# The start of a recursive matrix kernel: fewer warm-up products, whole-tile normalising, and another order of transposes, copies and sums

## The chip, the cores and the metric

The kernel runs on one core of a Trainium2 chip. Its metric is the device time of one execution in microseconds (us), the median of several runs. The core has five engines that run side by side, each through its own list of instructions in order: TensorE multiplies matrices (in the profile PE, with the loads of its stationary operand apart as PEld), VectorE (DVE) and ScalarE (ACT) compute element by element and can read TensorE's result banks in PSUM, GpSimd (POOL) computes on SBUF only, and SyncE (SP) issues the transfers between HBM and SBUF. An engine that waits for another holds everything behind it in its own list.

## The reference

The input x is 2 x 1024 tokens of 512 values, in float32. What is computed, cut to its core:

```python
xn = layernorm(x)                          # no weights, eps 1e-5
s = einsum('bsk,nk->bsn', xn, weight * block_mask)        # 512 x 512, blocks of 32 x 32
nx = xn * rsqrt(mean(xn**2) + 1e-5) * ln_w
h = silu(einsum('bsh,ih->bsi', nx, gate_w)) * einsum('bsh,ih->bsi', nx, up_w)   # 1792 rows each
ffn = einsum('bsi,hi->bsh', h, down_w)
out = x + s * silu(ffn)
```

## The kernel before, in words

The tokens are cut into four groups t of 512; each group is four tiles i of 128 tokens x 512 values. A tile is loaded with the tokens on the partitions, normalised there, and turned by TensorE in 128 x 128 pieces: `transpose(t, c, i)` turns chunk c (128 of the 512 values) of tile i into a quarter of the bank `pt[t, c]`. A full bank is copied to SBUF by ScalarE (`evacuate`, L163) and is then an operand, `raw[c, t]`, of 128 x 512. For a float32 product of 128 x 512 the trace shows two matmul records, 0.43 us apart.

Products are saved by two levels of a Strassen-Winograd scheme. The outer level makes seven block instances q out of a large product, each inner instance seven products m of 128 x 512 instead of eight. The operands 1, 2 and 3 are data as they are; the operands 5, 6, 7 and 4 are differences, made for the tokens by `inner_b` (for instances 1 and 2 of the first stage by VectorE straight out of the banks `pt[1, c]`) and for the weights by `inner_a` on GpSimd. Products are accumulated in the banks x, y and z of an instance; `seed`, `snap` and `total` (L350 to L373) copy or add what stands in them at given points, partly on ScalarE, partly on VectorE. A bank can only be written on when it has been read: so a copy or a sum decides when TensorE may go on.

There are eight groups g of weights: seven of gate and up weights, each 256 rows, and one of the masked weights. The instances 1 and 2 of all groups come first. They need only the tokens of t = 0 and 1, and so instance j = 0 (g 0, q 1) and j = 1 (g 0, q 2) start as soon as these are ready. Then come the instances 6, 5, 7, 3 and 4 of all groups, and at last the product with the down weights.

No scheduler decides the order. Every piece of work is entered by `at(pos, function, arguments)` with a position by hand; at the end the list is sorted by position and written out, so each engine's order is the order of the positions. A position is a slot of TensorE in the steady stream; instance j has the slots 7j and on, and `T(us)` turns an estimated time at the start into a position. `EARLY` holds positions of the first products (j, m) and of totals (j, "z") that differ from the rule; (j, 0) is the position of `seed`. The framework adds the waits that the data and the banks ask for, and between two engines that use one bank also where both only read: the one that comes later in the order waits.

The start, in the order of the code: SP loads tiles t = 0, weights of group 0, tiles t = 1, weights of group 1, and so on. TensorE is kept busy with products of an identity matrix that nobody reads (`warm`, L702). VectorE takes the statistics of each tile (L125, L126), works out a factor and an offset per token (`factors`: L139, a square root on ScalarE at L140, a reciprocal L136 and L137), and normalises tiles 2 and 3 in place (L146) while ScalarE does tiles 0 and 1 (L148), each in two halves of 256 columns. Then come transposes, copies and the first products for t = 0, and the same for t = 1. GpSimd multiplies the weights of group 0 by ln_w (L262) and forms their sums (L97, the helper `add`, which stands for sums on every engine). For group 1 ScalarE does this multiplication (`scale_a`, L264).

Of the kernel before, what the change touches and what calls it, by code (L numbers as in the profile page):

```python
# [15 lines left out]
W = 512  # L16
# [15 lines left out]
def tile_masked_linear_gated_ffn(  # L32
# [33 lines left out]
    EARLY = {}  # L66

    def at(pos, fn, *args):
        events.append((pos, len(events), fn, args))
# [23 lines left out]
    def bank(tag, name):  # L93
        return ps.tile([P, W], F32, tag=tag, name=name, bufs=PSB[tag])
# [4 lines left out]
    dve, pool, act = nc.vector, nc.gpsimd, nc.scalar  # L99
# [28 lines left out]
    def factors(t):  # L128


        scl = small.tile([P, TT], F32, tag="scl", name=f"scl_{t}")
        nb = small.tile([P, TT], F32, tag="nb", name=f"nb_{t}")
        stat[t] = (scl, nb)

        def last():
            nc.vector.reciprocal(scl, scl)  # L136
            nc.vector.scalar_tensor_tensor(nb, agg[:, t, :, 0], -1.0, scl, ALU.mult, ALU.mult)  # L137

        return [lambda: nc.vector.tensor_scalar(scl, agg[:, t, :, 1], 1.0 + EPS, EPS * EPS, ALU.mult, ALU.add),  # L139
                lambda: nc.scalar.activation(scl, scl, AF.Sqrt), last]  # L140
# [443 lines left out]
    def down_instance(o, q, where_, prior, dest, after):  # L584
# [78 lines left out]
        if last_set:  # L663
            at(where_(17) + 0.1, base_of_last)
            for part, pos in zip(parts, (where_(23), where_(24), where_(25))):
# [8 lines left out]
    where = {gq: j for j, gq in enumerate(order)}  # L674
    N = len(order)
    END = 7 * N
    T = lambda us: (us - 14.0) / 0.86
    EARLY.update({(0, 1): T(10.4), (0, 2): T(11.3), (1, 1): T(12.1), (1, 2): T(13.0), (0, 0): T(11.5), (1, 0): 4.3,
                  (0, "z"): 3.26, (1, "z"): 4.9})
    SILU = 26.2  # L680
    at(T(-10), constants)
    at(T(-10), load_x, 0)
    at(T(-10), lambda: nc.scalar.dma_start(lnw_sb, ln_w))

    at(T(-10), lambda: nc.gpsimd.tensor_copy(mem[:, F["a1"], 0:1], xt[0, 0][:, 0:1]))
    for K in range(2):
        at(T(-10), load_a, 0, K)
    at(T(-10), load_x, 1)
# [6 lines left out]
    def plan(pos, step, todo):  # L695
        for i, fn in enumerate(todo):
            at(pos + step * i, fn)


    def warm(n, b):  # L700
        for _ in range(n):
            nc.tensor.matmul(b[:, :P], ident, ident, start=True, stop=True, skip_group_check=True)  # L702

    at(T(1.4), lambda: warm(26, bank("V", "idle")))
    for t, p, step in ((0, T(7.1), 0), (1, T(12.5), 0), (2, 36.0, 1.2), (3, 36.1, 1.2)):
        plan(p, step, factors(t))
    for i in range(TT):
        half = act if i < 2 else dve
        at(T(3.7 + 0.82 * i), stats, 0, i)
        at(T(9.35 + 0.82 * i), stats, 1, i)  # L710
        for h, cols in enumerate((slice(0, W // 2), slice(W // 2, W))):
            at(T(7.95 + 0.9 * h + 0.4 * (i % 2)), normalise, 0, i, half, cols)
            at(T(13.45 + 0.9 * h + 0.4 * (i % 2)), normalise, 1, i, half, cols)
        for c in range(KC):
            at(T((8.9, 9.3, 9.8, 11.0)[c] + 0.05 * i), transpose, 0, c, (2, 3, 0, 1)[i], "XYYX"[c])
            at(T((14.35, 14.8, 15.25, 16.2)[c] + 0.05 * i), transpose, 1, c, (2, 3, 0, 1)[i], "XVVV"[c])
    at(T(6.0), scale_a, 0, 0, pool)
    at(T(6.1), scale_a, 0, 1, pool)
    for c in range(KC):
        at(T((9.75, 10.3, 10.85, 12.05)[c]), evacuate, 0, c, act)  # L720
        at((5.6, T(15.6), 6.0, 3.14)[c], evacuate, 1, c, act)
    for pos, q, m, eng in ((1.1, 1, 5, dve), (1.87, 1, 6, dve), (2.56, 1, 7, dve), (3.95, 2, 5, dve), (2.7, 1, 4, pool),
                           (4.6, 2, 6, dve), (7.2, 2, 7, dve), (5.0, 2, 4, pool)):
        at(pos, inner_b, q, m, eng)
    for q in (1, 2):
        for k in (0, 1):
            for n in (0, 1):
                at(8, outer_b, q, k, n, None)
    at(2.1, scale_a, 1, 0)
    at(5.2, scale_a, 1, 1)  # L730
    for i in range(TT):
        at(14.0 + 2.5 * i, stats, 2, i)
# [28 lines left out]
    for g in range(G + 1):  # L761
        p, rest = 7 * where[g, 1], 7 * where[g, BLOCKS[0]]
# [43 lines left out]
    def D(o):  # L806
        return lambda k: free[25 * o + k] if 25 * o + k < 25 * len(DOWN) else free[25 * o + k - 1] + 1
# [6 lines left out]
    for o, q in enumerate(DOWN):  # L814
# [24 lines left out]
        for k in range(4):  # L839
            pos = END + (-6, -4.8, 2, 4)[k] if o == 0 else D(o - 1)(10) + 2.5 * k  # L840
# [84 lines left out]
```

## Time and profile before

| | us |
|---|---|
| median of 3 runs (513.14 to 514.0) | 513.15 |
| profiled execution | 513.17 |
| span of its trace | 511.4 |
| TensorE busy in the span | 505.8 (99%) |
| VectorE | 380.4 (74%) |
| GpSimd | 340.9 (67%) |
| ScalarE | 182.6 (36%) |

The profile is of one execution. A row of the timeline gives the start and the length, both in us, the engine and the line of the code, the operation with its output and input, and in brackets how long the engine stood idle before it and who ended that. Several instructions of a kind that follow each other are put in one row (x4). A row of busy time by stretch gives the stretch, its length, and for PE, PEld, DVE, ACT and POOL the busy time and the number of instructions, then the clock that TensorE was granted, the busy share of the transfer engines, and GB/s.

### The profile page before, as it was taken

What the parts mean: (1) busy time and instruction counts of PE and PEld (TensorE: products, weight loads), DVE (VectorE), ACT (ScalarE), POOL (GpSimd) and SP (SyncE); (2) the same over time, 40 slices, a digit from 0 to 9 for tenths busy, and PEclk for the clock granted to TensorE, in tenths of its full rate; (3) what the DMA queues carried; (4) which work ended last, traced back from release to release, by engine and by line L of the source; (5) the groups of instructions that cost most, each with busy time, mean ns of one, the idle gap of its engine ahead of it and who ended that gap; (6) DMA issues with size and microseconds to landing.
All of it is one profiled execution on the core that took longest, in us unless ns stands there. A gap on an engine that the chain in (4) does not pass through costs nothing. (4 is left out here: it accounts for less than half of the span.)

```text
span 511.4 us, 4943 instructions
## 1 busy us (share of the span) xinstructions
PE 505.8 (99%) x1269; PEld 231.8 (45%) x1269; DVE 380.4 (74%) x590; ACT 182.6 (36%) x348; POOL 340.9 (67%) x283
## 2 busy tenths in 40 slices
PE   8999999999999999999999999999999999999997
PEld 8444444444444444444444444444444444444444
DVE  6878689876977969699696978968747645367736
ACT  4656754633536353353634433330100101001111
POOL 5522224994795968869597789976662754739960
PEclk9999999999999999999999999999999999999999
DMA  8436636369159386785948667499997698476472
GB/s 289 164 132 238 247 133 227 135 236 350 48 219 348 147 302 228 238 289 208 338 166 294 209 239 254 169 332 383 357 339 270 204 374 327 146 252 216 151 229 83
DMA packets 60460, 121.59 MB, mean 238 GB/s; under 512 B 5760, under 2 KB 13328, under 8 KB 58384
## 3 DMA queue, kind: packets, MB, share of 16 engines
q1 hardware_dynamic: 60288, 121.27, 66.8%
q8 instruction: 10, 0.16, 0.1%
q14 instruction: 18, 0.15, 0.1%
q10 hardware_dynamic: 144, 0.00, 0.0%
HBM read 75.11 MB, written 46.15 MB: 237 GB/s over the span
## 5 line engine op out<-in xcount | busy, mean ns | idle before, releaser
L97 POOL TENSOR_TENSOR mem<-mem 128x512 f32<-128x512 f32 (+4 forms) x245 | 305.2, 1267 | 135.4 <-ACT mem L264 36.5
L343 PE MATMUL x<-mem 128*128 128x512 f32 x448 | 213.6, 595 | 0.2 <-DVE mem L97 0.2
L343 PEld LDWEIGHTS x<-mem 128*128 128x128 f32 x448 | 83.7, 190 | 107.3 <-issue 86.9
L97 DVE TENSOR_TENSOR mem<-x,mem 128x512 f32<-128x512 f32 x137 | 92.5, 684 | 42.0 <-PE x L343 41.1
L343 PE MATMUL y<-mem 128*128 128x512 f32 x224 | 114.5, 593 | 0.3 <-DVE mem L97 0.3
L97 DVE TENSOR_TENSOR mem<-mem 128x512 f32<-128x512 f32 (+3 forms) x60 | 74.7, 1252 | 7.8 <-PE dx L591 4.3
L591 PE MATMUL dx<-mem 128*128 128x512 f32 x174 | 78.3, 592 | 0.0
L97 DVE TENSOR_TENSOR mem<-y,mem 128x512 f32<-128x512 f32 x96 | 65.6, 684 | 9.8 <-PE y L343 8.5
L343 PEld LDWEIGHTS y<-mem 128*128 128x128 f32 x224 | 42.2, 190 | 53.0 <-issue 47.8
L350 ACT COPY z<-x 128x512 f32<-128x512 f32 x54 | 30.9, 573 | 97.9 <-PE x L343 92.2
L343 PE MATMUL z<-mem 128*128 128x512 f32 x112 | 57.3, 593 | 0.0
L591 PEld LDWEIGHTS dx<-mem 128*128 128x128 f32 x174 | 33.1, 190 | 41.6 <-issue 40.4
L591 PE MATMUL dy<-mem 128*128 128x512 f32 x98 | 44.5, 592 | 0.0
L409 ACT ACTIVATE gate<-mem 128x512 f32<-128x512 f32 x56 | 33.1, 601 | 25.3 <-DVE mem L97 20.9
L414 DVE TENSOR_TENSOR mem<-gate,mem 128x512 f32<-128x512 f32 x56 | 38.0, 681 | 5.1 <-POOL mem L97 4.3
L564 POOL TENSOR_TENSOR mem<-mem 128x512 f32<-128x512 f32 x16 | 25.0, 1570 | 15.3 <-DMA mem<-s_dram 15.2
L343 PEld LDWEIGHTS z<-mem 128*128 128x128 f32 x112 | 21.0, 190 | 24.9 <-issue 23.9
L574 ACT ACTIVATE silu<-mem 128x512 f32<-128x512 f32 x15 | 9.0, 602 | 64.6 <-DVE mem L97 48.3
L97 DVE TENSOR_TENSOR mem<-z,mem 128x512 f32<-128x512 f32 x41 | 28.0, 682 | 3.5 <-PE z L343 3.5
L591 PEld LDWEIGHTS dy<-mem 128*128 128x128 f32 x98 | 18.6, 190 | 23.4 <-issue 23.4
L97 DVE TENSOR_TENSOR mem<-dx,mem 128x512 f32<-128x512 f32 x16 | 11.0, 690 | 20.1 <-PE dx L591 20.1
L591 PE MATMUL dz<-mem 128*128 128x512 f32 x56 | 25.2, 592 | 0.0
(73 smaller groups left out, 289.2 us busy)
## 6 DMA issues: line engine op xcount, KB each, us to landing
h_dram<-mem SPq DMA_DIRECT2D x98, 256.0 KB, 2.1
mem<-h_dram SPq DMA_DIRECT2D x28, 768.0 KB, 6.2
mem<-in_gu SPq DMA_DIRECT2D x42, 256.0 KB, 3.7
acc_dram<-mem SPq DMA_DIRECT2D x8, 1024.0 KB, 4.2
mem<-acc_dram SPq DMA_DIRECT2D x8, 1024.0 KB, 6.7
mem<-in_x SPq DMA_DIRECT2D x16, 256.0 KB, 5.2
s_dram<-mem SPq DMA_DIRECT2D x16, 256.0 KB, 4.8
mem<-s_dram SPq DMA_DIRECT2D x16, 256.0 KB, 6.3
```

What stands on the lines that cost most here:

```text
L97: eng.tensor_tensor(o, a, b, op)
L343: nc.tensor.matmul(st[key], weights(g, q, m), operand(q, m), start=first and not (key == "z" and seeded), stop=True, skip_group_check=True)
L350: nc.scalar.copy(st["z"], st["x"])
L409: nc.scalar.activation(gate[key], t(), AF.Silu)
L414: nc.vector.tensor_mul(a(), gate[key], b())
L564: at_later.append(lambda: nc.gpsimd.tensor_tensor(s_tile, s_tile, rms_bc[t], ALU.mult))
L574: nc.scalar.activation(b[0][:, part], y[:, part] if source is None else source(), AF.Silu)
L591: nc.tensor.matmul(st[key], w(), b(), start=first and key != "z", stop=True, skip_group_check=True)
```

## The change

Everything that changes is in the table of positions at the start; no function is changed.

- The identity products are 20 instead of 26.
- VectorE normalises tiles 2 and 3 of t = 0 and of t = 1 in one instruction each of 128 x 512, instead of two halves. ScalarE keeps its halves.
- For t = 0 the four chunks are transposed in a row; before, the first product stood between the third chunk and the fourth. Within chunks 0 and 1 the tiles are taken in the order 2, 0, 1, 3 (t = 0) or 0, 2, 1, 3 (t = 1) instead of 2, 3, 0, 1.
- For t = 1 the y product of instance 0 stands after chunk 1 instead of after chunk 2, and the x product m = 6 stands between chunk 2 and chunk 3.
- ScalarE: the copy of x of instance 0 (`seed`, L354) moves from between the third and the fourth copy of t = 0 to after the first copy of t = 1. The copy of chunk 3 of t = 1 moves behind the copy of x (L361), and is now later than the sum `inner_b(2, 6)` on the same bank; the first `scale_a` of group 1 moves behind the copy of y.
- VectorE: the z total of instance 0 moves ahead of the sum `inner_b(1, 7)`; the z total of instance 1 ahead of `inner_b(2, 6)`, right after the sum of x of instance 1 (`seed`, L356).
- The orders of GpSimd and of SP stay as they are.

```diff
-    T = lambda us: (us - 14.0) / 0.86
-    EARLY.update({(0, 1): T(10.4), (0, 2): T(11.3), (1, 1): T(12.1), (1, 2): T(13.0), (0, 0): T(11.5), (1, 0): 4.3,
-                  (0, "z"): 3.26, (1, "z"): 4.9})
+    T = lambda us: (us - 13.4) / 0.86
+    EARLY.update({(0, 1): T(10.2), (0, 2): T(11.1), (1, 1): T(12.0), (1, 2): T(12.9), (0, 0): 1.8, (1, 0): 4.3,
+                  (0, "z"): 2.5, (1, "z"): 4.6})
...
-    at(T(1.4), lambda: warm(26, bank("V", "idle")))
-    for t, p, step in ((0, T(7.1), 0), (1, T(12.5), 0), (2, 36.0, 1.2), (3, 36.1, 1.2)):
+    at(T(1.4), lambda: warm(20, bank("V", "idle")))
+    for t, p, step in ((0, T(7.1), 0), (1, T(12.2), 0), (2, 36.0, 1.2), (3, 36.1, 1.2)):
         plan(p, step, factors(t))
     for i in range(TT):
-        half = act if i < 2 else dve
         at(T(3.7 + 0.82 * i), stats, 0, i)
-        at(T(9.35 + 0.82 * i), stats, 1, i)
-        for h, cols in enumerate((slice(0, W // 2), slice(W // 2, W))):
-            at(T(7.95 + 0.9 * h + 0.4 * (i % 2)), normalise, 0, i, half, cols)
-            at(T(13.45 + 0.9 * h + 0.4 * (i % 2)), normalise, 1, i, half, cols)
+        at(T(8.9 + 0.82 * i), stats, 1, i)
+        for t, p in ((0, T(7.75)), (1, T(13.0))):
+            if i >= 2:
+                at(p + 0.6 * (i - 2), normalise, t, i, dve)
+                continue
+            for h, cols in enumerate((slice(0, W // 2), slice(W // 2, W))):
+                at(p + 1.04 * h + 0.52 * i, normalise, t, i, act, cols)
         for c in range(KC):
-            at(T((8.9, 9.3, 9.8, 11.0)[c] + 0.05 * i), transpose, 0, c, (2, 3, 0, 1)[i], "XYYX"[c])
-            at(T((14.35, 14.8, 15.25, 16.2)[c] + 0.05 * i), transpose, 1, c, (2, 3, 0, 1)[i], "XVVV"[c])
+            at(T((8.85, 9.3, 9.75, 9.95)[c] + 0.05 * i), transpose, 0, c, ((2, 0, 1, 3), (2, 3, 0, 1))[c // 2][i], "XYYX"[c])
+            at((T(14.0), T(14.3), 2.1, 4.05)[c] + 0.01 * i, transpose, 1, c, ((0, 2, 1, 3), (2, 3, 0, 1))[c // 2][i], "XVVV"[c])
...
     for c in range(KC):
-        at(T((9.75, 10.3, 10.85, 12.05)[c]), evacuate, 0, c, act)
-        at((5.6, T(15.6), 6.0, 3.14)[c], evacuate, 1, c, act)
-    for pos, q, m, eng in ((1.1, 1, 5, dve), (1.87, 1, 6, dve), (2.56, 1, 7, dve), (3.95, 2, 5, dve), (2.7, 1, 4, pool),
-                           (4.6, 2, 6, dve), (7.2, 2, 7, dve), (5.0, 2, 4, pool)):
+        at(T((9.65, 10.2, 10.8, 11.4)[c]), evacuate, 0, c, act)
+        at((5.6, 1.75, 6.0, 5.1)[c], evacuate, 1, c, act)
+    for pos, q, m, eng in ((1.3, 1, 5, dve), (1.9, 1, 6, dve), (3.1, 1, 7, dve), (3.95, 2, 5, dve), (2.7, 1, 4, pool),
+                           (4.9, 2, 6, dve), (7.2, 2, 7, dve), (5.0, 2, 4, pool)):
         at(pos, inner_b, q, m, eng)
...
-    at(2.1, scale_a, 1, 0)
+    at(3.05, scale_a, 1, 0)
```

## The prediction

> **What bounds the kernel now.** I read the page's busy times first, then busy time by stretch, then TensorE's waits, then the timeline of the first 26 us.
>
> ```profile
> PE 505.8 (99%) x1269; PEld 231.8 (45%) x1269; DVE 380.4 (74%) x590; ACT 182.6 (36%) x348; POOL 340.9 (67%) x283
> ...
> 20.00:25.00 5.00, 4.66 (x11) 1.84 (x11) 4.90 (x9) 2.31 (x6) 3.96 (x5) 1.00 0.00 0
> 25.00:100.00 75.00, 75.00 (x201) 34.88 (x200) 62.39 (x113) 46.92 (x90) 27.89 (x31) 1.00 0.52 190
> 100.00:500.00 400.00, 399.85 (x929) 175.48 (x928) 292.07 (x420) 119.78 (x228) 299.07 (x224) 1.00 0.71 251
> ```
>
> From 25 to 500 us TensorE stands still for 0.15 us in all. Its order there is the same in both kernels, so whatever the start gains or loses reaches the end, and the change is priced at one mark: the start of the first product of the third block instance (x, j=2), now 25.13 us. After it only the end of the program follows, which doesn't change. In 20 to 25 us VectorE is the busiest (4.90 of 5).
>
> ```profile
> 1.35 8.79 PEld L702 LDWEIGHTS idle<-ident 128*128 128x128 f32 x52 [1.35 <-POOL ident masks.py:199]
> 7.74 1.76 DVE L146 TENSOR_SCALAR mem<-mem,scl,nb 128x256 f32<-128x256 f32 x4
> 7.79 2.07 ACT L148 ACTIVATE mem<-mem,nb,scl 128x256 f32<-128x256 f32 x4 [0.50 <-DVE nb L137]
> 9.43 0.67 DVE L125 BATCH_NORM_STATS2 st<-mem 128x6 f32<-128x512 f32 x1
> 10.05 1.34 PEld L155 LDWEIGHTS pt<-ident,mem 128*128 128x128 f32 x12
> 12.73 0.38 DVE L139 TENSOR_SCALAR scl<-agg 128x4 f32<-128x4 f32 x1
> 13.10 0.59 ACT L163 COPY mem<-pt 128x512 f32<-128x512 f32 x1
> 13.83 0.18 DVE L136 RECIPROCAL scl<-scl 128x4 f32<-128x4 f32 x1 [0.71 <-ACT scl L140]
> 14.24 1.59 DVE L146 TENSOR_SCALAR mem<-mem,scl,nb 128x256 f32<-128x256 f32 x4
> 16.07 0.69 DVE L97 TENSOR_TENSOR mem<-pt,mem 128x512 f32<-128x512 f32 x1 [0.25 <-PE pt L155]
> 17.12 0.69 DVE L97 TENSOR_TENSOR mem<-pt,mem 128x512 f32<-128x512 f32 x1 [0.36 <-ACT mem L163]
> 21.55 1.10 PE L343 MATMUL y<-mem 128*128 128x512 f32 x2 [0.34 <-DVE mem L97]
> 22.51 0.68 DVE L97 TENSOR_TENSOR mem<-x,mem 128x512 f32<-128x512 f32 x1
> 23.29 0.69 DVE L97 TENSOR_TENSOR mem<-y,mem 128x512 f32<-128x512 f32 x1
> 25.13 1.88 PE L343 MATMUL x<-mem 128*128 128x512 f32 x4
> ```
>
> To be seen: (1) the identity products hold TensorE to 10.05, though the first normalised halves are there before 9; (2) the statistics of the second 512 tokens (9.43) start when VectorE has done its halves of the first; (3) their square root waits in ScalarE behind the copy at 13.10, so the reciprocal stands 0.71; (4) from 17.12 VectorE runs one sum every 0.60, ten rows and nine steps to the total at 22.51, which frees the bank for TensorE's last product of instance 0. That row is the path.
>
> **What the Trainium skill says.** "PSUM — Partial Sum Buffer", section on bank collisions: two engines must not touch one bank at once, reads included, and schedulers add a dependency. The trace agrees: the sum at 17.12 waits for ScalarE's copy of the bank it only reads. "SBUF — State Buffer", section "Who interferes with whom": VectorE's two-port modes (tensor_scalar among them) and GpSimd share a port pair as an exclusive lock. The trace shows a cost but no full block: beside GpSimd's 0.93 us instructions the half tiles start 0.43 to 0.47 apart, the first 0.33. "VectorE: DVE Perf Modes", section on the DRAIN: a result that the next instruction reads needs a wait. The trace: 22.51 to 23.29 is 0.78, not 0.60. "TensorE: Matmul & The Clock Gate", "What's actually happening": the clock is halved after an idle window of about 3.4 us; see the slower rival.
>
> **The change, part by part.** All "before" times are rows of the timeline.
>
> Six identity products fewer. 27 of the 52 weight loads lie in the first 5.85 us, 25 in the next 2.85, so the last twelve cost 12 x 0.114 = 1.4; the transposes may begin at 8.7. But tile 1's second half comes from ScalarE at 9.87 and ScalarE takes the first copy only after starting that half at 9.28 plus its 0.50 pace, 9.79 (before 10.80). Four copies at 0.49 end at 11.84; ScalarE is then free for the square root, so the 0.71 goes. Four chunks in a row: pt_3's transposes end at 10.8, first product at 10.58 (before 11.48), and four products of 0.86 end at 14.02 (before 15.43). TensorE thus has room; what it waits for next is normalised data.
>
> Whole tiles on VectorE. The timeline has the form later on, with GpSimd idle:
>
> ```profile
> 48.96 0.54 DVE L146 TENSOR_SCALAR mem<-mem,scl,nb 128x512 f32<-128x512 f32 x1
> 49.41 0.68 DVE L97 TENSOR_TENSOR mem<-y,mem 128x512 f32<-128x512 f32 x1
> ```
>
> It lasts 0.54 and the next starts after 0.45. Beside GpSimd a half cost some 0.13 more, so a whole tile starts the next after 0.45 (contention hidden) to 0.72 (paid per element); I take 0.57, and 0.66 for its duration. VectorE leaves at 7.74 + 1.14 = 8.88 instead of 9.43. Statistics go at 0.80: fourth at 11.28. Its load was issued at 6.15 and took 5.0, so it lands at 11.15: the transfer would allow only 0.13 more. L139 follows 0.91 later as before, 12.19. It lasts 0.17 (first tokens) or 0.38 (second, beside GpSimd); I take 0.38. Square root 12.60, reciprocal after 0.25, nb and normalise 0.41 on: 13.26, 0.98 earlier than 14.24.
>
> Second transposes. Tile 3 starts at 13.83, ends 14.49; weight load 0.09 later, product 0.11, its length 0.27: pt_0 complete at 14.96, first sum at 15.00 (before 16.07). pt_1 ends 15.40; ScalarE's last half starts 14.75 and ends 15.35; copy 15.44 to 16.02; second sum at 16.05, 1.07 earlier. pt_2's transposes now follow the y product, so TensorE idles some 0.8 before it. This costs nothing while VectorE is the path: the third sum of a bank, t2_5, needs pt_2 at about 17.3 and comes up at 17.9.
>
> VectorE's new order. Nine steps of 0.60 lead to the total of x (before 17.12 to 22.51). Two are lengthened. x_220's running sum now stands directly before z_226's total, which reads it: +0.18 (nothing to +0.18). The copy of pt_3 was before, and is now after, the sum t2_6 on its bank: t2_6 starts 16.05 + 3.60 + 0.18 = 19.83, ends 20.51, the copy ends 21.13, and t2_7, due 21.03, starts 21.16: +0.13 (nothing to +0.2). Total of x: 16.05 + 5.40 + 0.31 = 21.76, against 22.51: 0.75 earlier. TensorE's last product of instance 0, the y product and the mark follow as before.
>
> What queues behind that waiting copy on ScalarE, from about 18.7: the second scale_a of group 1 (two halves, 0.91), then copies of pt_0 and pt_2. GpSimd's first sums of group 1 start at 22.1, not 22.16 as before, and take 0.73; TensorE needs that sum at about 26: 3 us of slack, no cost. scale_a 1,0, one copy later than before, is waited for by no one sooner. The square root, the zero-cost moves of seeds (ScalarE's copy of x at 16.0 ends 16.5, before the z total at 16.65) and the earlier Y bank (z total ends at 16.05 + 3.00 + 0.18 + 0.68 = 19.9, TensorE comes at about 20.2; the 0.34 wait goes) need no more. SP's queue and GpSimd's order are unchanged.
>
> **Sum.** 513.17 (profiled run; span 511.4) less 0.75 is 512.42; the median shown is 513.15. Bounds: contention hidden and L139 short brings the normalise 0.13 + 0.21 earlier and shortens tile 3 by 0.24, but TensorE isn't free before 14.02, so pt_0 can't be complete before 14.65: gain at most 1.38 - 0.31 = 1.07, and 1.38 if neither lengthening bites. Full contention: L139 at 12.48, normalise 13.55, first sum 15.59, gain 0.48 - 0.31 = 0.17.
>
> **Rivals.** A measurement here can tell 0.2%, 1.03 us, from no change.
> - Forecast, gain 0.75: 512.4. Chance 0.50.
> - Cover holds: no port contention, or the two lengthenings hidden; gain 1.07 to 1.38, 511.9. For it: the first half at 7.74 ran at 0.33 although GpSimd had begun. Against: the later three. 0.25.
> - Eaten: full contention, gain 0.17, 513.0. For it: three halves of four. 0.12.
> - Slower, one mechanism: TensorE's clock. With fewer identity products the holes (0.8 us before the y product, some 0.8 before the last product of instance 0) might make it fall back. The weight loads stood 0.21 apart early and 0.11 after about 7.2 us: a slow pace exists. By the page's window and half rate, each slow window in the unbroken stretch after 25 us costs an estimated 1.7 us; one leaves 513.17 - 0.75 + 1.7 = 514.1, two give 515.8. It decides once a window of 3.4 us is mostly idle; my longest hole is 0.8. 0.13.
> That the change doesn't do what it says is ruled out by the two instruction orders: 20 products, two whole tiles, four chunks in a row.
>
> **Numbers.** Range 511.8 to 513.5: from the best bound to the eaten case, with a little beyond for launches (513.14 to 514.0 before); the clock case lies outside. Faster by over 0.2% (below 512.12) is the cover case and a tail of the forecast: 0.28. Slower: 0.13. Same: 0.59.
>
> **What would show it.** Right: weight loads of the transposes from about 8.7; whole tiles 0.57 apart; statistics from 8.9; normalise 13.3; first sum on pt_0 near 15.0, total of x near 21.8, mark near 24.4, no new hole after 25 us. Wrong: a total of x later than 22.5, weight loads 0.2 apart after 9 us, or GpSimd's first sums of group 1 after 25.

## The result, and the profile after

| | before | after |
|---|---|---|
| median, us | 513.27 (513.14 to 514.0, 4 runs) | 516.21 (515.01 to 516.37, 4 runs) |
| profiled execution, us | 513.17 | 515.01 |
| span of its trace, us | 511.4 | 513.2 |

The ratio of after to before is 1.0049, 95% interval 1.0031 to 1.0067: the changed kernel is slower. The profiled execution is the shortest of the four, so it shows only part of the loss; a later launch shows the rest.

The page's busy times of the kernel after:

```profile
PE 504.7 (98%) x1257; PEld 230.3 (45%) x1257; DVE 380.8 (74%) x586; ACT 182.4 (36%) x348; POOL 342.0 (67%) x283
```

Busy time by stretch of the kernel after:

```profile
20.00:25.00 5.00, 2.88 (x7) 0.94 (x5) 3.16 (x5) 2.35 (x5) 3.30 (x4) 1.00 0.00 0
25.00:100.00 75.00, 74.84 (x200) 34.97 (x201) 62.38 (x114) 45.69 (x87) 26.74 (x30) 1.00 0.52 190
100.00:500.00 400.00, 399.85 (x929) 175.46 (x928) 292.67 (x419) 121.09 (x232) 301.30 (x226) 1.00 0.71 251
```

The whole-program shares hardly move. The stretch from 20 to 25 us does: TensorE falls from 4.66 to 2.88 us busy and VectorE, which was the bound there, from 4.90 to 3.16. An engine that was the bound and now stands still has met a new wait. From 25 us on TensorE is as full as before (the 0.16 us that it lacks up to 100 us is the end of that hole). The mark, the first x product of the third block instance, lies at 26.96 instead of 25.13: 1.83 us, against 1.84 us between the two profiled executions. So the start holds the whole difference of these two executions, as the prediction assumed, with the opposite sign.

The timeline of the kernel after:

```profile
7.83 1.22 DVE L146 TENSOR_SCALAR mem<-mem,scl,nb 128x512 f32<-128x512 f32 x2
...
8.49 0.21 PEld L155 LDWEIGHTS pt<-ident,mem 128*128 128x128 f32 x2
...
8.97 0.68 DVE L125 BATCH_NORM_STATS2 st<-mem 128x6 f32<-128x512 f32 x1
...
10.27 0.69 DVE L125 BATCH_NORM_STATS2 st<-mem 128x6 f32<-128x512 f32 x1 [0.40 <-DMA mem<-in_x]
...
14.01 1.35 DVE L146 TENSOR_SCALAR mem<-mem,scl,nb 128x512 f32<-128x512 f32 x2
...
15.78 0.69 DVE L97 TENSOR_TENSOR mem<-pt,mem 128x512 f32<-128x512 f32 x1 [0.42 <-PE pt L155]
...
20.63 0.68 DVE L97 TENSOR_TENSOR mem<-pt,mem 128x512 f32<-128x512 f32 x1
...
21.34 0.58 ACT L163 COPY mem<-pt 128x512 f32<-128x512 f32 x1 [1.71 <-DVE mem L97]
...
21.83 0.91 ACT L264 ACTIVATE mem<-mem,lnw_sb 128x256 f32<-128x256 f32 x2
...
22.64 1.06 ACT L163 COPY mem<-pt 128x512 f32<-128x512 f32 x2
...
23.73 0.69 DVE L97 TENSOR_TENSOR mem<-mem,pt 128x512 f32<-128x512 f32 x1 [1.82 <-ACT mem L163]
24.33 0.68 DVE L97 TENSOR_TENSOR mem<-x,mem 128x512 f32<-128x512 f32 x1
...
25.16 1.10 PE L343 MATMUL x<-mem 128*128 128x512 f32 x2 [2.28 <-POOL mem L97]
...
26.96 1.88 PE L343 MATMUL x<-mem 128*128 128x512 f32 x4
```

Read it from the end. TensorE stands 2.28 us before the product at 25.16. Its bracket names GpSimd, but the product starts 0.15 us after VectorE's total of x (24.33 + 0.68 = 25.01). The same 0.15 lies between total and product in the experiments below where the bracket names VectorE. The name in a bracket is only the last event of a wait for several. The total is late because the sum before it, t2_7 at 23.73, stood 1.82 us. (t2_6 and t2_7 are what `inner_b(2, 6)` and `inner_b(2, 7)` make, t2_4 is GpSimd's `inner_b(2, 4)`, and pt_2 stands for the bank `pt[1, 2]`. In the code t2_7 is the SBUF copy of pt_3 less the bank pt_2. So it needs the copy of pt_3 as its operand, and it must also wait for the copy of pt_2 where that comes earlier in the order, since both read this bank.) It was released by ScalarE's copies: the row at 22.64 is two copies, of pt_0 and then of pt_2, the bank that t2_7 reads, and ends at 23.70. This copy stands in ScalarE's list behind two halves of `scale_a` (21.83) and the copy of pt_3 (21.34), and that one waited 1.71 us for VectorE's sum t2_6 on its bank. The circle is VectorE, ScalarE, VectorE: t2_6, the copy of pt_3, the weights, the copies of pt_0 and pt_2, t2_7.

In the kernel before, the same two copies and the same sum stand like this:

```profile
20.72 1.06 ACT L163 COPY mem<-pt 128x512 f32<-128x512 f32 x2
...
21.92 0.67 DVE L97 TENSOR_TENSOR mem<-mem,pt 128x512 f32<-128x512 f32 x1
```

The copies end at 21.78, 0.14 us before t2_7, and no wait shows.

### The profile page after: what moved, and what is told of

Same layout as the page of the kernel before. It is cut to its first block, busy times and chain, and to the rows that moved or that the text cites. A ratio compares the mean times of both kernels' runs of the same rounds, so it can differ in the third digit from the quotient of the medians.

```text
span 513.2 us, 4915 instructions
## 1 busy us (share of the span) xinstructions
PE 504.7 (98%) x1257; PEld 230.3 (45%) x1257; DVE 380.8 (74%) x586; ACT 182.4 (36%) x348; POOL 342.0 (67%) x283
```

## The experiments

All were timed in five rounds, each beside the kernel before on the same chip. In each profile two rows separate the causes. Up to VectorE's first sum out of pt_0 lies what loads, statistics and normalising decide; from there to the total of x lies mainly what the order of copies and sums decides. The split is sharp to some 0.2 us only: i1_before_loads has the order of before and takes 6.24 us between, not 6.44.

| profiled run | first sum | total of x | between | mark | median, us | ratio to before, 95% |
|---|---|---|---|---|---|---|
| before | 16.07 | 22.51 | 6.44 | 25.13 | 513.27 | |
| after | 15.78 | 24.33 | 8.55 | 26.96 | 516.21 | 1.0049 [1.0031, 1.0067] |
| a_again | 15.06 | 23.61 | 8.55 | 27.41 | 516.33 | 1.0053 [1.0037, 1.0068] |
| f_fill | 16.02 | 24.57 | 8.55 | 27.20 | 515.15 | 1.0033 [1.0021, 1.0045] |
| e2_scale_behind | 15.70 | 23.46 | 7.76 | 26.08 | 514.59 | 1.0028 [1.0018, 1.0039] |
| e4_before_copy_late | 16.64 | 24.40 | 7.76 | 27.02 | 514.81 | 1.0032 [1.0021, 1.0044] |
| e1_copy_first | 15.51 | 22.25 | 6.74 | 24.87 | 513.39 | 1.0005 [0.9997, 1.0013] |
| e3_pt2_behind | 15.78 | 22.57 | 6.79 | 25.19 | 513.46 | 1.0006 [0.9997, 1.0014] |
| h1_orders | 15.55 | 22.35 | 6.80 | 24.97 | 512.93 | 0.9996 [0.9988, 1.0004] |
| h2_loads | 15.06 | 21.86 | 6.80 | 24.48 | 512.83 | 0.9992 [0.9984, 1.0001] |
| i1_before_loads | 16.11 | 22.35 | 6.24 | 24.97 | 513.05 | 1.0003 [0.9995, 1.0011] |
| i2_halves | 16.32 | 23.10 | 6.78 | 25.72 | 513.55 | 1.0013 [1.0006, 1.0019] |

The mark lies 2.61 to 2.63 us after the total of x in all of them but a_again.

**1. The copy ahead of the sum on its bank.** In the kernel after, the sum t2_6 and GpSimd's t2_4 move behind ScalarE's copy of pt_3.

```diff
-                           (4.9, 2, 6, dve), (7.2, 2, 7, dve), (5.0, 2, 4, pool)):
+                           (5.15, 2, 6, dve), (7.2, 2, 7, dve), (5.17, 2, 4, pool)):
```

> The changed kernel with one dependency turned round: the copy of pt_3 reads the bank before the sum t2_6 does; ScalarE's own order stays. Theory A (the copy of pt_3 waits for t2_6 and holds four instructions of ScalarE, among them the copy of pt_2 for which t2_7 waits): ScalarE's 1.71 us wait before that copy is gone, t2_7 follows the y total within 0.2 us instead of 1.82, TensorE's 2.28 us hole shrinks below 0.6, time about 513.3. Rival B (TensorE's clock or something after 25 us costs the time): the hole goes but the time stays above 514.5. Rival C (the order of the sums alone): t2_7 still waits over 1 us.

Measured: 513.39 us. The timeline of this kernel:

```profile
19.26 0.59 ACT L163 COPY mem<-pt 128x512 f32<-128x512 f32 x1
...
20.55 1.07 ACT L163 COPY mem<-pt 128x512 f32<-128x512 f32 x2
...
21.65 0.69 DVE L97 TENSOR_TENSOR mem<-mem,pt 128x512 f32<-128x512 f32 x1
```

No bracket is left at t2_7, and the stretch between falls from 8.55 to 6.74. t2_7 still comes right behind the copies (20.55 + 1.07 = 21.62), but they are done 2.1 us sooner. One pair of readers in the other order brings back some 2.6 us (2.94 less 0.30, each against its own kernel before). By itself this doesn't say whether t2_7 waited for the copy of pt_3 (as the prediction had it) or for one behind it; the next two tell that.

**2. Only the weights behind.** The copies stay as they are after the change; the second `scale_a` moves behind those of pt_0 and pt_2.

```diff
-    at(5.2, scale_a, 1, 1)
+    at(6.1, scale_a, 1, 1)
```

> The changed kernel, the second scale_a of group 1 behind the copies of pt_0 and pt_2 instead of ahead of them. Theory A: the copies come 0.8 us earlier, t2_7 and all behind it too, time about 0.8 under the changed kernel, 515.4 by its median or 514.2 by its fastest launch; GpSimd starts group 1's sums later without TensorE waiting for them. Rival B: no change of over 0.3 us.

Measured: 514.59 us. The timeline of this kernel:

```profile
21.26 1.56 ACT L163 COPY mem<-pt 128x512 f32<-128x512 f32 x3 [1.70 <-DVE mem L97]
...
22.85 0.69 DVE L97 TENSOR_TENSOR mem<-mem,pt 128x512 f32<-128x512 f32 x1 [1.03 <-ACT mem L163]
```

t2_7 waits 1.03 us instead of 1.82, that is 0.79 less for 0.91 us of ScalarE's work taken out of the way. Part of the wait is this work, which touches none of t2_7's data: a queue behind the waiting copy. The median falls by more, 1.62 us; in none of its seven launches is the mean clock below 0.999, and 5 and 6 show what that is worth.

**3. Only the copies of pt_0 and pt_2 behind the sum.** The copy of pt_3 and `scale_a` stay; the other two come after t2_7.

```diff
-        at((5.6, 1.75, 6.0, 5.1)[c], evacuate, 1, c, act)
+        at((7.25, 1.75, 7.3, 5.1)[c], evacuate, 1, c, act)
```

> The changed kernel, the copies of pt_0 and pt_2 behind the sum t2_7, so that t2_7 waits only for the copy of pt_3. Theory A: t2_7 at about 21.95 instead of 23.73, time about 1.8 under the changed kernel, 513.2 by its fastest launch, 514.4 by its median. Rival B: no change of over 0.3 us.

Measured: 513.46 us. The timeline of this kernel:

```profile
21.34 0.59 ACT L163 COPY mem<-pt 128x512 f32<-128x512 f32 x1 [1.70 <-DVE mem L97]
...
21.96 0.69 DVE L97 TENSOR_TENSOR mem<-mem,pt 128x512 f32<-128x512 f32 x1
...
22.63 1.06 ACT L163 COPY mem<-pt 128x512 f32<-128x512 f32 x2
...
23.40 1.10 PE L343 MATMUL x<-mem 128*128 128x512 f32 x2 [0.51 <-DVE mem L97]
...
26.91 1.02 PE L343 MATMUL y<-mem 128*128 128x512 f32 x2
```

The copy of pt_3 still stands 1.70 us and still ends at 21.93, and t2_7 comes 0.03 after it, at 21.96: 1.77 earlier than in the kernel after, from the same first sum. So what t2_7 had waited for was the copy of its own bank pt_2. GpSimd, which the bracket at the hole named, isn't the cause: its row of sums starts at 21.45 in both kernels, and the product comes 1.76 us earlier here. What is left is the wait for the copy of pt_3, t2_7's operand: the small delay that the prediction priced.

**4. The wait alone, in the kernel before.** Only the copy of pt_3 moves to where the change has it; normalising, transposes and totals are those of before.

```diff
-        at((5.6, T(15.6), 6.0, 3.14)[c], evacuate, 1, c, act)
+        at((5.6, T(15.6), 6.0, 5.1)[c], evacuate, 1, c, act)
```

> The kernel before with one edit of the change alone: the copy of pt_3 at position 5.1, behind t2_6. Theory A: the copy waits until about 20.8 us, t2_7 starts at about 23.2 instead of 21.9, TensorE gets a hole of about 1.2 us, time about 514.5. Rival B: within 0.3 us of the kernel before.

Measured: 514.81 us against 513.09. The timeline of this kernel:

```profile
21.41 0.58 ACT L163 COPY mem<-pt 128x512 f32<-128x512 f32 x1 [0.82 <-DVE mem L97]
...
22.70 1.06 ACT L163 COPY mem<-pt 128x512 f32<-128x512 f32 x2
...
23.79 0.69 DVE L97 TENSOR_TENSOR mem<-mem,pt 128x512 f32<-128x512 f32 x1 [1.22 <-ACT mem L163]
```

The one moved copy makes the kernel before slower by 0.32% and lengthens its stretch between from 6.44 to 7.76, 1.32 us. t2_7 is late by 1.30 (due at 21.89 + 0.60 = 22.49) instead of the 1.90 of the kernel after, where it was due at 21.83: in the order of before one sum more, 0.60 us, lies between t2_6 and t2_7. Its first sum is late too (16.64), for another reason: the statistics of the second tokens waited 0.91 us for their load. The median is 1.72 above that of before; how much of the 0.40 beyond the stretch is such lateness of loads, one profile can't tell.

**5. The changed kernel again.** It was run once more because the median lies 1.2 us above the profiled execution, which the new wait doesn't explain.

> The changed kernel itself once more, beside the kernel before. Theory A alone: the hole of about 2.3 us makes it about 515.0 in every launch, some 1.9 above the kernel before. Rival D (the hole is long enough for TensorE's clock to fall back in most launches): median about 516.2, with single launches near 515.0.

Measured: 516.33 us (514.57 to 517.42). Busy time by stretch of this run, TensorE alone:

```profile
22.00:24.00 2.00, 0.17 (x1) 1.00 0.00 0
24.00:25.00 1.00, 0.55 (x2) 1.00 0.00 0
25.00:25.50 0.50, 0.50 (x2) 0.54 0.12 33
25.50:26.00 0.50, 0.50 (x2) 0.50 0.00 0
26.00:28.00 2.00, 2.00 (x3) 0.50 0.31 131
28.00:28.50 0.50, 0.50 (x2) 0.55 1.27 524
28.50:29.00 0.50, 0.50 (x2) 1.00 0.87 295
```

And its timeline:

```profile
13.28 1.36 DVE L146 TENSOR_SCALAR mem<-mem,scl,nb 128x512 f32<-128x512 f32 x2
15.06 0.69 DVE L97 TENSOR_TENSOR mem<-pt,mem 128x512 f32<-128x512 f32 x1 [0.42 <-PE pt L155]
...
23.01 0.69 DVE L97 TENSOR_TENSOR mem<-mem,pt 128x512 f32<-128x512 f32 x1 [1.82 <-ACT mem L163]
...
24.45 1.47 PE L343 MATMUL x<-mem 128*128 128x512 f32 x2 [2.28 <-POOL mem L97]
25.71 1.92 PE L343 MATMUL y<-mem 128*128 128x512 f32 x2
...
29.65 1.02 PE L343 MATMUL y<-mem 128*128 128x512 f32 x2
```

The hole is the same 2.28 us (22.17 to 24.45). TensorE starts again at full clock, but soon the granted clock is 0.50, for 3.4 us: the means of 0.54 and 0.55 put the two edges near 25.04 and 28.45. The y product takes 1.92 instead of 1.02. From the end of the hole to the second product of the third instance it is 5.20 us (24.45 to 29.65), in e3_pt2_behind 3.51 (23.40 to 26.91): 1.69 us lost to the clock. In the two measurements of the changed kernel, 6 of 10 launches had a mean clock of 0.995 or 0.996, and they took 516.04 to 517.42 us; the other four, at 0.999 or 1.0, took 514.57, 514.89, 515.01 and 516.18. The last of these isn't explained. The second thing to see: in this launch the loads were early, and VectorE's front is where the prediction put it.

**6. The hole filled.** To test the clock apart from the wait, nine identity products that nobody reads stand in the hole of the kernel after.

```diff
+    at(11.5, lambda: warm(9, bank("Z", "fill")))
```

> The changed kernel with nine identity products more, put where TensorE stands still for 2.28 us, into the free bank Z; nothing else moves. They last about 2 us (9 x 0.23) and should end before the product that waits. Theory A alone: time as the changed kernel measured beside it, within 0.3 us. Rival D: about 1.2 us under it, near 515.0, since TensorE doesn't stand still.

Measured: 515.15 us (514.78 to 515.33), clock 0.999 or 1.0 in all five launches. The timeline of this kernel:

```profile
22.96 2.17 PE L702 MATMUL fill<-ident 128*128 128x128 f32 x18
...
25.41 1.10 PE L343 MATMUL x<-mem 128*128 128x512 f32 x2 [0.27 <-POOL mem L97]
```

t2_7 is no sooner (the stretch between is 8.55 again), and yet the median falls by 1.18 us against a_again on the same chip, and the spread from 2.85 to 0.55. This much of the loss was the clock. The rest, 515.15 against 513.27, holds the wait.

**7. More order put right.** On e1_copy_first, the z total of instance 1 moves back to its old place, and the first copy of t = 1 behind the second sum.

```diff
-                  (0, "z"): 2.5, (1, "z"): 4.6})
+                  (0, "z"): 2.5, (1, "z"): 5.3})
-        at((5.6, 1.75, 6.0, 5.1)[c], evacuate, 1, c, act)
+        at((5.6, 1.95, 6.0, 5.1)[c], evacuate, 1, c, act)
```

> The kernel with the copy of pt_3 first, and two more orders: the z total of instance 1 behind t2_6 again, so that it no longer follows the sum that it reads, and t2_6's sister t1_6 ahead of the copy of pt_1. By the rows: 0.18 and about 0.25 us earlier at the total of x, 513.0 against 513.4 for the kernel with the copy first. If the path is the loads of the second tokens alone, the gain is the same, as both lie behind them; if it is TensorE, none.

Measured: 512.93 us, near the time expected, but not to be told from before, and not by the rows expected. The two moves bring nothing in the stretch between (6.80 against 6.74): t2_6 now waits 0.37 us for the copy of pt_3.

**8. The second tokens sooner.** On top of that, SP issues the tiles t = 1 before the second half of the weights of group 0.

```diff
-    for K in range(2):
-        at(T(-10), load_a, 0, K)
+    at(T(-10), load_a, 0, 0)
     at(T(-10), load_x, 1)
+    at(T(-10), load_a, 0, 1)
```

> As the one before, and the second 512 tokens loaded ahead of the second half of group 0's weights. If the landing of these tokens is the path (statistics start when the first tile lands): they land 0.4 to 0.8 us earlier, time about 0.4 lower, 512.6. If GpSimd's weights become the path (its scaled second half comes about 2 us later): third product after 13.3 us instead of 12.3, hidden as long as it stays before 13.6; otherwise no gain or a loss of up to 1 us.

Measured: 512.83 us, 0.9992 [0.9984, 1.0001], the best of all, but its interval still reaches no change. The timeline of this kernel:

```profile
7.78 1.17 DVE L146 TENSOR_SCALAR mem<-mem,scl,nb 128x512 f32<-128x512 f32 x2
...
8.87 0.68 DVE L125 BATCH_NORM_STATS2 st<-mem 128x6 f32<-128x512 f32 x1
...
13.21 1.14 DVE L146 TENSOR_SCALAR mem<-mem,scl,nb 128x512 f32<-128x512 f32 x2
15.06 1.49 DVE L97 TENSOR_TENSOR mem<-pt,mem 128x512 f32<-128x512 f32 x2 [0.71 <-PE pt L155]
...
21.86 0.68 DVE L97 TENSOR_TENSOR mem<-x,mem 128x512 f32<-128x512 f32 x1
```

Statistics follow the whole tiles at once, with no wait for a load, and the total of x comes 0.65 before that of the kernel before.

**9. The loads alone, in the kernel before.** The edit of 8 in the kernel before.

> The kernel before with one edit: SP issues the second 512 tokens of x ahead of the second half of group 0's weights. Theory A (VectorE's order bounds the start of before, and the loads only sometimes): the statistics of the second tokens already begin at 9.4 when VectorE has done its halves, so nothing is gained: total of x near 22.5, mark 25.0 to 25.2, time 512.9 to 513.4, ratio 0.9995 to 1.0005. Rival B (the late landing of those tokens costs the kernel before something in most launches): faster by 0.2 to 0.6 us, ratio 0.9988 to 0.9996, as h2_loads is against its own kernel before. Rival C: GpSimd's second weight half lands later and delays its first sums, slower, 513.6 or more.

Measured: 513.05 against 513.0, 1.0003 [0.9995, 1.0011]: by itself the order of loads brings nothing measurable; the interval leaves room for a gain of 0.26 us at most. VectorE is busy with halves up to 9.45 there, so theory A stands, but for the smallest gains of rival B.

**10. Halves again.** h2_loads with VectorE's normalising in halves, so that the fourth half of t = 0 falls behind the first statistic of t = 1.

```diff
-            if i >= 2:
-                at(p + 0.6 * (i - 2), normalise, t, i, dve)
-                continue
             for h, cols in enumerate((slice(0, W // 2), slice(W // 2, W))):
-                at(p + 1.04 * h + 0.52 * i, normalise, t, i, act, cols)
+                at(p + 1.04 * h + 0.52 * (i % 2), normalise, t, i, act if i < 2 else dve, cols)
```

> h2_loads with VectorE's normalising in halves of 256 columns again (before's form), all else as there. Theory A (whole tiles were the gain of the change at the front): VectorE leaves the first tokens near 9.4 instead of 8.9 and the second 0.2 to 0.5 later: total of x 22.3 to 22.6 instead of 21.86, mark 24.9 to 25.2 instead of 24.48; time 513.2 to 513.6. Rival B (halves run beside GpSimd at the same cost per element, and what waits is the landing of the tokens): total of x within 0.2 of h2_loads, time 512.7 to 513.0.

Measured: 513.55 us, 1.0013 [1.0006, 1.0019] to its own kernel before; this interval lies apart from that of h2_loads, which was timed on another chip. The timeline of this kernel:

```profile
8.53 1.19 DVE L146 TENSOR_SCALAR mem<-mem,scl,nb 128x256 f32<-128x256 f32 x3
9.64 0.68 DVE L125 BATCH_NORM_STATS2 st<-mem 128x6 f32<-128x512 f32 x1
...
10.45 0.38 DVE L146 TENSOR_SCALAR mem<-mem,scl,nb 128x256 f32<-128x256 f32 x1
...
14.42 1.97 DVE L146 TENSOR_SCALAR mem<-mem,scl,nb 128x256 f32<-128x256 f32 x4
```

The sign is theory A's, and the time lies in its range; the total of x, 23.10, lies beyond its 22.3 to 22.6. But this launch began its first half 0.75 later than h2_loads, and one half waited behind a statistic, so neither the 1.24 us between the two totals of x nor the difference of the medians is the price of the form alone. In the second tokens the form is worth little: from the start of normalising to the first sum it is 1.90 us in halves and 1.85 in whole tiles. With halves the sum follows them at once; with whole tiles VectorE is done sooner and then stands 0.71 us for TensorE (the row at 15.06 in 8).

## Why the prediction was wrong

The forecast was 512.4 and the range 511.8 to 513.5; the median was 516.21. It put the total of x at 21.76; it came at 24.33, 2.57 later. This splits into 0.78 at the first sum and 1.79 in the stretch between, and the clock adds to it in most launches.

- **The step that failed** is the term in VectorE's new order: "t2_7, due 21.03, starts 21.16: +0.13 (nothing to +0.2)". Due at 21.23 + 0.60 = 21.83 in this launch, t2_7 started at 23.73: +1.90. The prediction let it wait for the copy of pt_3, its operand, alone. It also reads the bank pt_2, and the copy of pt_2 comes earlier in the order, so it waits for that one, with 0.91 us of `scale_a` and the copy of pt_0 in between. The next paragraph of the prediction had listed this very queue ("the second scale_a of group 1 (two halves, 0.91), then copies of pt_0 and pt_2") and asked only what GpSimd would miss, not what VectorE would. In the kernel before the two copies were done 0.14 us before t2_7, so no wait in the profile told of the dependency; the section on bank collisions of the Trainium skill's "PSUM — Partial Sum Buffer" that the prediction itself cited did. e3_pt2_behind is the kernel that was priced: there the wait is 0.13 (21.23 + 0.60 to 21.96), and the stretch between 6.79 against 21.76 - 15.00 = 6.76 forecast. e4_before_copy_late shows the same wait without the rest of the change.
- **The slower rival** had the clock right, which takes the second part of the loss, but not the wait, which is in no rival. From the Trainium skill's "TensorE: Matmul & The Clock Gate", section "What's actually happening", it took an idle window of about 3.4 us, and it let the clock fall once such a window is mostly idle. It was held unlikely because its longest hole was 0.8 us. The failed step made a hole of 2.28 us. In a_again the 3.4 us before the clock fell (21.63 to 25.04) hold all of it, so they are mostly idle, and the slow stretch cost 1.69 us there, near the estimated 1.7 of the rival. The trace of this launch thus agrees with the rival's rule, and what was mis-sized is the hole; in the profiled launch of after the same hole left the clock at 1.00, which stays open. The filled hole shows a worth of 1.18 us at the median. The early weight loads 0.21 us apart are no evidence for this rival: the profile gives a granted clock of 1.00 there too.
- **The gain ahead of the first sum** was right in its sum and wrong in taking the loads as fixed. In a_again normalising starts at 13.28 and the first sum at 15.06, against 13.26 and 15.00 forecast. In the profiled launch of after the second statistic waited for its tile to 10.27, where the forecast's pace gives 8.88 + 0.80 = 9.68, and the offset (L137) took 0.45 us beside GpSimd instead of 0.16; so 14.01 and 15.78. The prediction looked at the landing of the fourth tile alone and found 0.13 us to spare; here the second tile cost about 0.5 us (8.97 + 0.80 = 9.77 against 10.27). So the forecast gain isn't there even without the failed step: in the profile of e3_pt2_behind the first sum comes 0.29 earlier than before, the stretch between takes 0.35 more, and the median is 0.37 above that of before.
- **Right**: the identity products end at 8.49 (8.7 forecast), whole tiles start 0.53 and 0.68 apart (0.57), the square root no longer waits behind a copy, the z total after its running sum costs 0.18 more (e3_pt2_behind: 0.78 instead of 0.60), nothing happens after 25 us but the clock, and GpSimd's first sums of group 1 start before 25.

The account of the medians, each against its own kernel before: the order of e3_pt2_behind, without the long wait, 0.37 us (not told from nothing); the wait, as the filled hole has it, brings this to 1.88, so 1.51; the clock 1.18 more. The sum is 3.06 for a_again, as it must be for steps from run to run, and the first measurement gave 2.94. The profiles give the wait 1.76 us (8.55 less 6.79) where the medians give 1.51; the runs don't say what makes the rest.

## What to carry to other kernels

When a piece of work on one engine is made to wait, list everything that stands behind it in that engine's list, and for each entry every engine that reads or writes the same bank afterwards, readers among them: the wait is handed on to all of these. A dependency that never shows as a wait in the kernel before may have been met there with 0.14 us to spare. And an idle hole of TensorE has a second price beyond its length; where it can't be closed, products that nobody reads are a cheap test of how much of the loss that is.

## What the runs showed of the hardware that wasn't expected

- A hole of 2.28 us before a full stretch was enough to take TensorE's clock to 0.50 for 3.4 us (25.04 to 28.45 in a_again), in one of the two profiled launches of the same kernel and not in the other. The clock fell 0.6 us after TensorE had started again. Holes of 1.48 us (e2_scale_behind) and 1.15 us (e4_before_copy_late) left it at 0.999 or 1.0 in all 13 launches. So the window of about 3.4 us that the prediction took need not be idle throughout. Where the limit lies between 1.48 and 2.28, and why the other launches with the hole of 2.28 us kept their clock, wasn't tried. Two of 21 launches of i2_halves also show 0.996, at 515.26 and 514.97 us, with only shorter holes in its profiled launch (the longest 0.93 us, ahead of the first transposes). They weren't profiled, so what did it there stays open.
- The loads of the second tokens land at very different times from launch to launch: the first statistic had no wait at 8.78 in a_again, and waited for its load to 9.37 in e1_copy_first, 9.73 in e2_scale_behind and 10.35 in e4_before_copy_late. A gain of 0.5 us that relies on a load being there is then a gain in some launches only.
